# A fourth place in the ring of residual rows of a gated cross-attention block

## The chip, the cores and the metric

The kernel runs on one core of a Trainium2 chip. The metric is the device time of one execution in microseconds (us). Five engines work side by side, each through its own instructions in a fixed order: TensorE (PE, with PEld its weight loads), VectorE (DVE), ScalarE (ACT), GpSimd (POOL) and SyncE (SP), which here only issues DMAs. They wait for one another through semaphores.

## What is computed

The reference is one block of a Flamingo-like network. `x` has 16 sequences of 224 tokens of 512 numbers; the context has 16 sequences of up to 750 rows of 384, of which a mask drops some.

```python
x = x + tanh(g_xattn) * xattn(layernorm(x), ctx, mask, W_q, W_k, W_v, W_o, b_o)
x = x + tanh(g_ffn)   * ffn(layernorm(x), w1, b1, w2, b2)
# xattn: 8 heads of 64; softmax(q k^T / 8, masked) v, then @ W_o + b_o
# ffn:   h = gelu(bitlinear(x, w1, b1)); bitlinear(h, w2, b2)
# bitlinear: rows rms-normalised and rounded to 8 bits, weights rounded to -1, 0, 1
```

Both `x +` are residual adds: the first needs the rows of `x` once more, long after they were normalised for the attention.

## The kernel before, in words

The kernel first sorts the sequences by how many context rows the mask keeps, so that each of 16 attention slots has a fixed width (192, 128 or 64 rows). The work that matters here is in `compact_path`.

The attention goes slot by slot, one sequence of 224 tokens in each. The rest goes by tiles of 128 tokens, two tiles to a pair: 28 tiles, 14 pairs, numbered 0 to 13. Within slot s a list of pieces is merged from three streams by estimated costs: the attention of slot s (`attention_pieces`), the preparation of slots s+1 and s+2 (normalising, gathering context, keys, queries), and `flow`, the work on pairs: the output projection of the newest pair, the first ffn matmul of the pair before it, the second one of the pair before that.

A pair lives like this. `residual(i)` takes a tile `y` of two times 128 rows of 512 numbers, fetches the rows of `x` into it with two indirect DMAs (line 808, through the helper `fetch_x`) and adds `bo`, the projection's bias, on GpSimd (line 1245). `project(i, k)` adds the attention's output on DVE (line 1255). `normalise` makes the 8-bit rows and adds `b2` to `y` on GpSimd (line 1312). `up`, `gelu` and `down` are the ffn: `hp` (line 1333), `h`, the rounded rows `hq`, their transpose `hqT` by a DMA of SP (line 1377), and `fp` (line 1475). `store(i, k)` adds the ffn's output to `y` on DVE (line 1488) and sends the 128 rows out with an indirect DMA of GpSimd (line 1494); the last two pairs go out by SP.

`y` comes from a ring: the tag "y" of the pool `rows` has `bufs` places, and a new tile takes the place of the tile `bufs` pairs before it. The first instruction that writes into a place waits until the store of its old rows has landed. The pool opens when the raw weights of the ffn have been used up, and takes their memory; beside "y" it has tags "hq" (the places of `fx` and `hq`, three) and "hqT" (two).

In the attention, `scores(s, n)` makes the scores `sim` on PE, the exponentials `p` on ACT and the reciprocals `rec` of their sums on DVE, and then scales `p` on GpSimd (line 1140). `turn_probs` transposes the scaled `p` on PE (`ptp`, line 1163, and `ptr`, line 1170).

The pieces are not the last word on the order. When the program is built, a scheduler settles the order of instructions on each engine: an instruction may move ahead of others on its engine if what it needs is there sooner. In the built program of before, GpSimd fetches the rows of pairs 0, 1 and 2 together, as soon as the pool `rows` has its memory, and those of pair i directly behind the second store of pair i-3, whose place they take.

Of the kernel before, what the change touches and what calls it, by code (L numbers as in the profile page):

```python
# [8 lines left out]
F32 = mybir.dt.float32  # L9
# [725 lines left out]
def compact_path(ctx, tc, sh, x, context, out, late_loads, stages):  # L735
# [4 lines left out]
    P = 128  # L740
    B, S, D = x.shape
# [65 lines left out]
    def fetch_x(dst, t):  # L807
        nc.gpsimd.indirect_dma_start(
            out=dst,
            out_offset=None,  # L810
            in_=x_rows,
            in_offset=bass.IndirectOffsetOnAxis(ap=token(t), axis=0),
            bounds_check=B * S - 1,
            oob_is_err=False,
        )
# [420 lines left out]
    late = {}  # L1236

    def residual(i):

        f = pairs[i] = {}  # L1240
        f["y"] = y = late["rows"].tile([P, 2, D], F32, tag="y", name=f"y_{i}", bufs=3)
        for k in range(2):
            fetch_x(y[:, k, :], 2 * i + k)
        for k in range(2):
            nc.gpsimd.tensor_tensor(y[:, k, :], y[:, k, :], sh.bo, ALU.add)
# [471 lines left out]
    for s in range(B):  # L1717
# [8 lines left out]
        if s < 2:  # L1726
            flow = weight_pieces(s)
        else:
            complete = 256 * (projected + 1) <= S * s
            if projected == 0:  # L1730
                nc.gpsimd.tensor_scalar(sh.bo, sh.bo, sh.tgates[:, 0:1], None, ALU.mult)
                nc.gpsimd.tensor_scalar(sh.b2, sh.b2, sh.tgates[:, 1:2], None, ALU.mult)
            if complete:
                flow.append((0.0, lambda i=projected: residual(i)))
            if s == B - 1:
                flow += last_slot(projected)
            elif raised < projected:
                flow += up_pieces(raised)
                raised += 1
            if complete and s < B - 1:  # L1740
                flow += project_pieces(projected)
                projected += 1
                if lowered < raised:
                    flow += down_pieces(lowered)
                    lowered += 1
# [26 lines left out]
    }  # L1772
    i = NPAIR - 1
    residual(i)
    with tc.issue_after(late["av"]), tc.issue_after(late["rounded"]):
        for k in range(2):
# [4 lines left out]
    f = pairs[i - 1]  # L1781
# [80 lines left out]
```

## Time and profile before

| | |
|---|---|
| runs of the kernel before | median 727.38 us of 3 (724.31 to 728.94) |
| the profiled execution | 728.15 us, span of its instructions 726.0 us |
| busy, PE / DVE / ACT / POOL | 674.0 / 493.1 / 413.0 / 391.5 us |
| mean granted TensorE clock | 0.986 |
| residual fetches, line 808 into `y` | 28, median 1035 ns on GpSimd, first at 103.5 us, last at 650.7 us |
| their adds of `bo`, line 1245 | 28, median 1273 ns |
| row stores by GpSimd, line 1494 | 24, median 1115 ns |

A row of a timeline has the start in us from the span's start, the duration in us, the engine, the line of the kernel, the operation with output and input, the count, and in brackets the idle time of the engine before it and what ended that idle time. A row of waits has engine, line and what was waited for, then the total in us, how many times, and the longest. "issue" means that nothing in the profile explains the gap. `p`, `y` and other names stand for all buffers of that name.

### The profile page before, as it was taken

The page shows a single profiled execution, that of the slowest core. Times are in us where ns is not written, and L with a number is a line of the kernel's source. Part 1 is how long each engine was busy: PE and PEld are TensorE (multiplying, and loading weights), DVE is VectorE, ACT ScalarE, POOL GpSimd, SP SyncE. Part 2 cuts the span into 40 slices and gives each one's busy share as a digit, 9 for nine tenths or more (in the row PEclk, how much of TensorE's full clock was granted, in tenths as well). Part 3 has the DMA queues.
Part 4 walks back from the last instruction along what each step waited for, and adds up shares of the span by engine and source line. Part 5 has one row for each costly group of instructions (what it writes and reads, how often), then busy time and mean ns, then how long its engine had stood idle before and what let it go on. Part 6 is the DMA issues. An engine that isn't in the chain of part 4 may idle for free.

```text
span 726.0 us, 11445 instructions
## 1 busy us (share of the span) xinstructions
PE 674.0 (93%) x3917; PEld 430.3 (59%) x3917; DVE 493.1 (68%) x1296; ACT 413.0 (57%) x974; POOL 391.5 (54%) x545
## 2 busy tenths in 40 slices
PE   4996899999989999999798999999999999999984
PEld 3774686765656555656565566566666556554432
DVE  5495666777477476675575966757859393869993
ACT  2556664377484672674566646837556563656642
POOL 5584478553494444735646656457554535276441
PEclk9998999999999999999999999999999999999998
DMA  7784031022232122213232331312313222142211
GB/s 239 288 277 162 0 84 51 18 60 53 68 85 60 54 59 59 85 29 90 60 45 90 83 78 46 66 44 74 82 46 59 73 54 77 30 99 47 69 33 49
DMA packets 80146, 56.74 MB, mean 78 GB/s; under 512 B 68208, under 2 KB 68352, under 8 KB 79952
## 3 DMA queue, kind: packets, MB, share of 16 engines
q1 hardware_dynamic: 72336, 31.22, 18.1%
q0 software_dynamic: 7744, 24.71, 11.1%
q8 instruction: 33, 0.54, 0.3%
q14 instruction: 33, 0.27, 0.1%
HBM read 32.06 MB, written 7.34 MB: 54 GB/s over the span
## 4 chain that ended last, share of the span: by engine, by line
PE 56%; DVE 13%; issue 13%; POOL 10%; ACT 4%; DMA 2%; POOLq 0%; DVEq 0%
PE qp L1066 10%; PE op L1252 9%; PE hp L1333 8%; PE fp L1475 6%; PE kp L946 4%; PE sim L1106 4%; PE vp L962 4%; PE ptp L1163 3%; PE av L1188 2%; DVE a L1369 2%; POOL p L1140 2%; POOL out_dram L1494 1%; DVE hq L1372 1%; PE xnp L1045 1%; POOL y L1312 1%
## 5 line engine op out<-in xcount | busy, mean ns | idle before, releaser
L1140 POOL TENSOR_TENSOR p<-p,rec 112x768 f32<-112x768 f32 (+2 forms) x64 | 78.6, 1230 | 74.9 <-DVE rec L1139 28.8
L1130 ACT ACTIVATE p<-p,nm 112x192 f32<-112x192 f32 (+2 forms) x256 | 104.7, 412 | 9.9 <-DVE nm L1120 6.8
L1066 PE MATMUL qp<-xnT,wq_sb 128*128 128x224 f32 x512 | 105.3, 359 | 0.6 <-issue 0.6
L1252 PE MATMUL op<-wo_sb,xoT 128*128 128x512 f32 x224 | 104.0, 599 | 0.0
L1475 PE MATMUL fp<-w2T,hqT 128*128 128x512 fp8e4 x448 | 101.4, 379 | 2.4 <-ACT hqT L1355 1.3
L1333 PE MATMUL hp<-w1T,xqT 128*128 128x512 fp8e4 x416 | 99.7, 384 | 3.0 <-DVE nm L1120 1.3
L1066 PEld LDWEIGHTS qp<-xnT,wq_sb 128*128 128x128 f32 x512 | 97.1, 194 | 6.4 <-issue 4.1
L1341 DVE SCALAR_TENSOR_TENSOR h<-hp,c,b_bc 128x1024 f32<-128x1024 f32 x52 | 66.5, 1280 | 43.8 <-PE hp L1333 43.5
L1120 DVE CUSTOM_DVE_ANT_0 p<-sim,mask 112x192 f32<-112x192 f32 (+2 forms) x224 | 56.0, 303 | 31.9 <-PE sim L1106 31.5
L1475 PEld LDWEIGHTS <-hqT 128*128 128x128 bf16 x448 | 42.7, 98 | 56.3 <-issue 5.3
L1369 DVE TENSOR_REDUCE a<-h 128x1 f32<-128x2048 f32 x26 | 59.3, 2281 | 20.3 <-ACT h L1366 20.1
L1333 PEld LDWEIGHTS <-xqT 128*128 128x128 bf16 x416 | 40.0, 98 | 47.6 <-issue 8.9
L1252 PEld LDWEIGHTS op<-wo_sb,xoT 128*128 128x128 f32 x224 | 40.6, 190 | 38.3 <-issue 35.9
L1488 DVE SCALAR_TENSOR_TENSOR y<-fp,c,y 128x512 f32<-128x512 f32 x28 | 20.8, 745 | 62.1 <-PE fp L1475 59.3
L1494 POOL DMA_INDIRECT out_dram<-y,token x24 | 27.6, 1148 | 58.0 <-DVE y L1488 53.6
L946 PE MATMUL kp<-ctxT,wk_sb 128*128 128x192 f32 (+1 forms) x360 | 57.8, 308 | 0.0
L1382 ACT ACTIVATE h<-h 128x2048 f32<-128x2048 f32 x25 | 47.7, 1909 | 17.1 <-DVE hq L1372 11.8
L1312 POOL TENSOR_TENSOR y<-y,b_bc 128x512 f32<-128x512 f32 x28 | 37.0, 1322 | 37.2 <-DVE fx L1292 36.9
L781 ACT COPY pT<-ptp 128x448 f32<-128x448 f32 (+1 forms) x62 | 32.2, 535 | 42.2 <-PE ptp L1163 41.4
L946 PEld LDWEIGHTS kp<-ctxT,wk_sb 128*128 128x128 f32 x360 | 52.4, 193 | 5.5 <-issue 3.8
L1106 PE MATMUL sim<-kT,qT 64*112 64x192 f32 (+2 forms) x512 | 51.5, 314 | 1.8 <-issue 0.9
L781 ACT COPY qT<-qp 128x448 f32<-128x448 f32 x29 | 15.4, 532 | 65.9 <-PE qp L1066 60.3
(199 smaller groups left out, 1249.3 us busy)
## 6 DMA issues: line engine op xcount, KB each, us to landing
raw<-in_L_ffn_w_dram SPq DMA_DIRECT2D x16, 512.0 KB
wq_sb<-in_L_xattn_W_q_dram SPq DMA_DIRECT2D x1, 1024.0 KB
b_bc<-in_L_ffn_b_dram SPq DMA_DIRECT2D x1, 1024.0 KB
wk_sb<-in_L_xattn_W_k_dram SPq DMA_DIRECT2D x1, 768.0 KB
wv_sb<-in_L_xattn_W_v_dram SPq DMA_DIRECT2D x1, 768.0 KB
wo_sb<-in_L_xattn_W_o_dram SPq DMA_DIRECT2D x1, 512.0 KB
wo_sb<-in_L_xattn_W_o_dram SPq DMA_DIRECT2D x2, 256.0 KB
out_dram<-y SPq DMA_DIRECT2D x2, 256.0 KB
```

The lines of the kernel that those rows point to most:

```text
L946: nc.tensor.matmul(pk[:, p - p0, :], lhsT=sh.wk[:, c, p * P : (p + 1) * P], rhs=st["ctxT"][:, c, :cap], start=(c == 0), stop=(c == NC - 1),)
L1066: nc.tensor.matmul(pq[:, i, :], lhsT=sh.wq[:, d, (p + i) * P : (p + i + 1) * P], rhs=st["xnT"][:, d, :], start=(d == 0), stop=(d == ND - 1),)
L1106: nc.tensor.matmul(sim[:, j, i, :cap], lhsT=st["qT"][j * DH : (j + 1) * DH, p, q * TQ : (q + 1) * TQ], rhs=keys["kT"][j * DH : (j + 1) * D ...
L1120: nc.vector.tensor_tensor_reduce(out=probs[:, h, :cap], in0=sim[:, j, i, :cap], in1=keys["mask"][:, first + j * begin : first + j * begin ...
L1130: nc.scalar.activation(probs[:, h, :cap], probs[:, h, :cap], AF.Exp, bias=nmax, scale=-1.0, accum_out=total[:TQ, h : h + 1],)
L1140: nc.gpsimd.tensor_tensor(probs[:, :, first : first + cap], probs[:, :, :cap], rec[:TQ].unsqueeze(2).to_broadcast([TQ, 4, cap]), ALU.mult,)
L1252: last = nc.tensor.matmul(po, lhsT=xoT[:, d, at : at + P], rhs=sh.wo[:, d, :], start=(d == 0), stop=(d == ND - 1))
L1333: last = nc.tensor.matmul(ph[:, n, :], lhsT=f["xqT"][:, k * ND + d, :], rhs=w1T[:, d, at : at + NB], start=(d == 0), stop=(d == ND - 1),)
L1341: nc.vector.scalar_tensor_tensor(h[:, cols], ph.rearrange("t i n -> t (i n)"), f["c1", k], sh.b1[:, cols], ALU.mult, ALU.add)
L1369: nc.vector.tensor_reduce(amax[:, k : k + 1], h, AX.X, ALU.max, apply_absolute_value=True)
L1382: nc.scalar.activation(f["h", k], f["h", k], AF.Square, accum_out=ss[:, k : k + 1])
L1475: last = nc.tensor.matmul(po, lhsT=f["hqT", k][:, n, :], rhs=w2T[:, n, :], start=(n == 0), stop=(n == NF - 1))
```

## The change

One number: the tag "y" of the pool `rows` has four places instead of three.

```diff
@@ residual(i) @@
         f = pairs[i] = {}
-        f["y"] = y = late["rows"].tile([P, 2, D], F32, tag="y", name=f"y_{i}", bufs=3)
+        f["y"] = y = late["rows"].tile([P, 2, D], F32, tag="y", name=f"y_{i}", bufs=4)
         for k in range(2):
             fetch_x(y[:, k, :], 2 * i + k)
```

A place is 4 KB in each of the 128 partitions. Pair i now takes the place of pair i-4 instead of pair i-3. The pool grows by one place, and the tags behind "y" lie one place further on. No computation is added or removed.

## The prediction

> **What bounds the kernel now.** I read the page first (busy shares, then the chain that ended last), then the waits, then the timeline of GpSimd (POOL) around the residual rows, and last TensorE (PE) beside it. The two lines of the page:
>
> ```profile
> PE 674.0 (93%) x3917; PEld 430.3 (59%) x3917; DVE 493.1 (68%) x1296; ACT 413.0 (57%) x974; POOL 391.5 (54%) x545
> ...
> PE 56%; DVE 13%; issue 13%; POOL 10%; ACT 4%; DMA 2%; POOLq 0%; DVEq 0%
> ```
>
> PE is busy for 674.0 of 726.0 us, so all its idle time together is 52 us. A microsecond taken from another engine counts only where PE was waiting for it, and one added counts only where PE comes to wait. The list of waits tells how GpSimd enters:
>
> ```profile
> PE ptp L1163 <- POOL p L1140: 16.9, 10, 5.6
> ...
> POOL y L808 <- DMA out_dram<-y,token: 20.4, 10, 2.3
> ```
>
> GpSimd stands 20.4 us in ten places before it may fetch residual rows, because the store of the rows that lie in the place hasn't landed. PE waits 16.9 us for the scaled probabilities `p` of line 1140, which GpSimd makes behind those fetches. One such place, in GpSimd's timeline (start, duration, what, idle before it):
>
> ```profile
> 192.97 1.11 POOL L1494 DMA_INDIRECT out_dram<-y,token  x1 [6.37 <-DVE y L1488]
> 196.13 1.06 POOL L808 DMA_INDIRECT y<-in_x_dram,token  x1 [2.05 <-DMA out_dram<-y,token]
> 197.50 1.02 POOL L808 DMA_INDIRECT y<-in_x_dram,token  x1 [0.31 <-issue]
> 199.62 1.27 POOL L1245 TENSOR_TENSOR y<-y,bo_bc 128x512 f32<-128x512 f32 x1 [1.11 <-DMA y<-in_x_dram,token]
> 200.85 1.46 POOL L1140 TENSOR_TENSOR p<-p,rec 112x768 f32<-112x768 f32 x1
> ```
>
> Store of pair 0, 2.05 us of standing, fetch of pair 3 into pair 0's place, 1.11 us of standing for the fetched rows, the add, and only then `p`. The change's words aim at the 2.05 us.
>
> [...]2.05 us from the end of the store's issue at 194.08 to the fetch. [...]the wait stands in GpSimd's queue, and everything behind it stands too. [...]the fetch of 196.13 shows 1.06 us, and its reader starts at 199.62, 3.49 us after the fetch began.
>
> **The change part by part.** The order in which the two programs issue their instructions decides this case. On PE, DVE, ACT and SP it is the same. On GpSimd only the residual fetches and their adds of `bo` move: every one stands one pair earlier. Before, the fetches of pairs 0, 1 and 2 stand together at the start, and pair i's stands directly behind the second store of pair i-3. After, pairs 0 to 3 stand together at the start, and pair i's stands directly behind the second store of pair i-4. With four places pair i takes the place of pair i-4. So the fetch again takes the place whose rows were sent in the instruction before it, and the wait for that store's semaphore is still on it. The extra place has been used to fetch a pair sooner, not to keep a place empty.
>
> 1. *The ten middle places* (pairs 0 to 9 stored): store, standing, two fetches, standing, add, `p` in the same order as in the excerpt, with the same tile sizes. Change: 0. Whether the rows are of pair 3 or 4 is nothing to `p`, and the first reader of the rows (line 1255) is a whole pair further off than before.
>
> 2. *The start* gets the two fetches and two adds of pair 3:
>
> ```profile
> 111.09 1.02 POOL L808 DMA_INDIRECT y<-in_x_dram,token  x1 [0.16 <-issue]
> 112.14 2.50 POOL L1245 TENSOR_TENSOR y<-y,bo_bc 128x512 f32<-128x512 f32 x2
> 114.80 1.01 POOL L808 DMA_INDIRECT y<-in_x_dram,token  x1 [0.16 <-issue]
> 115.85 1.29 POOL L1245 TENSOR_TENSOR y<-y,bo_bc 128x512 f32<-128x512 f32 x1
> 118.29 1.33 POOL L1245 TENSOR_TENSOR y<-y,bo_bc 128x512 f32<-128x512 f32 x1 [1.15 <-DVE keys L869]
> 119.58 1.46 POOL L1140 TENSOR_TENSOR p<-p,rec 112x768 f32<-112x768 f32 x1
> 121.90 1.47 POOL L1140 TENSOR_TENSOR p<-p,rec 112x768 f32<-112x768 f32 x1 [0.86 <-DVE mv_x L1011]
> ```
>
> The idle 1.15 us is the landing of the fetch of 114.80 (114.80 + 3.49 = 118.29), whatever name stands beside it. The new order is: fetch pair 2 second half, fetch 3, add 2, fetch 3, add 2, add 3, add 3, `p`. With 1.02 us and a gap of 0.31 or 0.16 for a fetch, 1.27 for an add and 3.49 from issue to landing: fetch at 114.80; fetch of 3 at 116.12 to 117.12; add to 118.45; fetch at 118.6 to 119.6; add at 119.65 to 120.95; third add to 122.2 (its rows landed at 119.6); fourth add, rows landed at 118.6 + 3.49 = 122.1, to 123.45. Then the two `p`: 123.45 to 124.9 and 124.95 to 126.4. They end 3.9 and 3.0 us later than before. It is 5.1 us of work (2 x 1.02, 2 x 0.25, 2 x 1.27), of which the 1.15 us of idle time takes up one.
>
> PE comes to the first of these `p` here:
>
> ```profile
> 121.50 0.92 PE L946 MATMUL kp<-ctxT,wk_sb 128*128 128x192 f32 x4
> 122.65 0.29 PE L1163 MATMUL ptp<-ident,p 112*128 112x112 f32 x1 [0.22 <-DVE y L1255]
> 122.77 1.48 PE L946 MATMUL kp<-ctxT,wk_sb 128*128 128x192 f32 x8
> 124.08 0.45 PE L1163 MATMUL ptp<-ident,p 112*128 112x112 f32 x3
> 124.38 0.35 PE L1170 MATMUL ptr<-ident,p 112*128 112x112 f32 x2
> 124.57 0.55 PE L1163 MATMUL ptp<-ident,p 112*128 112x112 f32 x4
> ```
>
> It can start at 124.9 + 0.06 (the gap from `p` to PE at 206.3) instead of 122.65: 2.3 us of new idle time. The second `p` is wanted at 124.57 + 2.3 = 126.9 and is done at 126.4: no more. What else is behind on GpSimd, the normalising of x tile 4 and the gather of context 5 (124.71 and 126.40 before), is read by PE from 148 on, and GpSimd then stood 3.38 us before its next `p` at 132.17. So only PE's 2.3 us are lost, and since the chain runs through PE from 122.93 to 152, nothing gives them back. Bounds: 1.2 us (landing sooner, adds lying better) to 3.9 us (the whole lateness of `p`).
>
> 3. *The end* loses the fetch of pair 13 behind the store of pair 10:
>
> ```profile
> 645.67 1.10 POOL L1494 DMA_INDIRECT out_dram<-y,token  x1 [0.17 <-DVE nm L1120]
> 648.79 1.06 POOL L808 DMA_INDIRECT y<-in_x_dram,token  x1 [2.01 <-DVE rec L1139]
> 649.87 0.62 POOL L1140 TENSOR_TENSOR p<-p,rec 112x256 f32<-112x256 f32 x1
> ```
>
> That `p` could go 1.1 us sooner (its `rec` ends at 648.72), and two adds at 652.29 and 654.94 vanish. But PE starts the transposes of this `p` at 650.92 directly behind line 1333's matmuls of 649.19, without idle time, and the next `p` at 658.19 waits for DVE. Gain 0, at most the 0.77 us that PE waits at 662.60.
>
> 4. *Places in memory*: the rows pool is 4 KB longer, so the buffers of tags hq and hqT lie one place on; the first transpose of `hqT` on SP gets one more wait, for GpSimd work long done by then. Cost 0. The page shows no effect of addresses; I keep half a microsecond either way.
>
> Sum: 0 + 2.3 - 0 + 0 = +2.3 us. The profiled execution took 728.15 us (span 726.0), so 730.45. The median of the runs is 727.38, 0.77 lower: 729.7.
>
> **The rivals.**
> - *A, forecast*: later `p` at the start costs PE 2.3 us, carried to the end: 729.7, its own range 728.5 to 731.5. Chance 0.55.
> - *B, hidden*: PE takes it back in later waits, or the freed GpSimd time at the end pays for it. For it: 52 us of PE idle time, 0.77 of them at 662.60. Against it: the later waits for `p` hang on stores that follow PE's own matmuls, so they move along. 727.4, give or take one. Chance 0.22.
> - *C, slower*: the crowding at the start also pushes the second `p`, the x tile and the gather, and PE pays the full 5.1 us of work plus a late stage behind it: 727.4 + 5 to 8, 733 to 735. For it: GpSimd is 74% busy from 100 to 120. Against it: GpSimd's 3.38 us of idle time before 132.17. Chance 0.15.
> - *D, faster, the change does what its words say*: the wait at the fetch is gone because the place was emptied a pair ago. Then each GpSimd stall of about 2 us goes, and PE gets back what it waits just behind, up to 2.05 a time: 1.07, 1.39, 1.47, 2.05 (of 3.65), 1.17, 0.35, 0.43, 1.02, together 8.95 us: 718.5. It decides as soon as more than 2.3 us of this come back. Against it: in the built order pair 4's fetch stands right behind the store of pair 0, with the wait. Chance 0.08.
>
> **How the numbers follow.** Likeliest is A: 729.7. The range goes from B's lower end to C's lower part, 726 to 733.5, which also holds the 0.6% by which the runs of before differ. About 1% (7.3 us) is what a measurement of this kernel tells from no change: over 1% faster is D alone, 0.08; over 1% slower is C's upper end and what the trace doesn't show of buffer places, 0.12; the rest, 0.80, lies within.
>
> **What would show it.** Right: in the profile after, ten waits of line 808 for `out_dram<-y`, still near 2.0 us each (about 20 in total); eight residual fetches before 125 us instead of six; PE waiting some 2 us for `p` of line 1140 near 123, and later stages later by that much. No residual fetch after 620. Wrong: if that wait is gone or far under 15 us in total, step 1 fails; if PE shows no wait near 123, step 2; if the time falls by over 3 us, something in the middle moves that the order doesn't show.

## The result, and the profile after

The changed kernel takes 730.86 us (median of 13 runs, 726.09 to 732.42); the kernel before, beside it, 726.4 us (13 runs, 723.4 to 728.94). The ratio is 1.0055, 95% interval 1.0037 to 1.0073: about 4.0 us slower, within 1%; the two medians alone differ by 4.5 us. The profiled execution took 731.07 us with a span of 729.0 us.

The two lines of the page after:

```profile
PE 677.2 (93%) x3917; PEld 433.4 (59%) x3917; DVE 498.2 (68%) x1296; ACT 412.8 (57%) x974; POOL 388.5 (53%) x545
...
PE 66%; DVE 14%; issue 6%; POOL 6%; ACT 4%; DMA 2%; POOLq 0%; DVEq 0%; ACTq 0%
```

PE is busy 3.2 us longer and DVE 5.1 us longer for the same numbers of instructions. Nothing was added to either, so something made instructions longer; 3.3 of DVE's 5.1 us are six instructions shown below. The list of waits after:

```profile
PE ptp L1163 <- POOL p L1140: 12.8, 10, 3.7
PE ptp L1163 <- DVE y L1255: 3.5, 1, 3.5
...
POOL y L808 <- DMA out_dram<-y,token: 20.5, 10, 2.2
```

The ten waits for a store are all there, 20.5 us against 20.4. The 3.5 us for DVE's line 1255 are new. (The longest wait for `p` before, 5.6 us, lay near 62 us, ahead of any residual row, where it is 1.5 us in the changed kernel and 2.8 us in `y3_late` below. Single executions differ there, so I compare stretches behind it.) The middle place in GpSimd's timeline, to be laid beside the one of before:

```profile
197.00 1.11 POOL L1494 DMA_INDIRECT out_dram<-y,token  x1 [6.36 <-DVE y L1488]
200.13 1.06 POOL L808 DMA_INDIRECT y<-in_x_dram,token  x1 [2.02 <-DMA out_dram<-y,token]
201.50 1.03 POOL L808 DMA_INDIRECT y<-in_x_dram,token  x1 [0.31 <-issue]
203.76 1.27 POOL L1245 TENSOR_TENSOR y<-y,bo_bc 128x512 f32<-128x512 f32 x1 [1.23 <-DMA y<-in_x_dram,token]
204.99 1.47 POOL L1140 TENSOR_TENSOR p<-p,rec 112x768 f32<-112x768 f32 x1
```

Same order, same 2.0 us: the fetch now is pair 4's, and it still stands right behind the store that empties its place. So the loss is made elsewhere, at the start. GpSimd there:

```profile
113.68 1.01 POOL L808 DMA_INDIRECT y<-in_x_dram,token  x1 [0.16 <-issue]
115.00 1.00 POOL L808 DMA_INDIRECT y<-in_x_dram,token  x1 [0.30 <-issue]
116.03 1.28 POOL L1245 TENSOR_TENSOR y<-y,bo_bc 128x512 f32<-128x512 f32 x1
117.47 1.11 POOL L808 DMA_INDIRECT y<-in_x_dram,token  x1 [0.16 <-issue]
118.60 3.71 POOL L1245 TENSOR_TENSOR y<-y,bo_bc 128x512 f32<-128x512 f32 x3
122.28 1.46 POOL L1140 TENSOR_TENSOR p<-p,rec 112x768 f32<-112x768 f32 x1
```

The first `p` ends at 123.74. TensorE should start its transpose 0.06 us later, but does so 1.4 us later still, and not for `p` (`kp` are the keys of a later slot, `qp` its queries):

```profile
120.70 0.92 PE L946 MATMUL kp<-ctxT,wk_sb 128*128 128x192 f32 x4
125.17 0.31 PE L1163 MATMUL ptp<-ident,p 112*128 112x112 f32 x1 [3.55 <-DVE y L1255]
125.29 2.77 PE L946 MATMUL kp<-ctxT,wk_sb 128*128 128x192 f32 x8
...
129.41 2.92 PE L1066 MATMUL qp<-xnT,wq_sb 128*128 128x224 f32 x14
```

It waits 3.55 us, and the eight `kp` matmuls behind take 2.77 us where they took 1.48. DVE's timeline says why line 1255 was late:

```profile
117.36 6.80 DVE L846 TENSOR_SCALAR ind<-place,upto 125x192 bf16<-125x192 bf16 x6
124.09 0.16 DVE L1139 RECIPROCAL rec<-sum 112x4 f32<-112x4 f32 x1
...
124.31 0.71 DVE L1255 SCALAR_TENSOR_TENSOR y<-op,tgates,y 128x512 f32<-128x512 f32 x1
```

Six small instructions, the indicators with which a later context's rows are selected, took 6.80 us (3.48 us before). The view of line 846 alone, in the stretch around it (shortest/median/longest in ns), shows that one of them took nearly all of it, here in the changed kernel,

```profile
L846 DVE TENSOR_SCALAR ind<-place,upto x6: 253/254/5907, 117.4 to 123.9; 125x192 bf16<-125x192 bf16 x6
```

and here in the kernel before:

```profile
L846 DVE TENSOR_SCALAR ind<-place,upto x6: 251/253/1499, 118.2 to 121.4; 125x192 bf16<-125x192 bf16 x6
```

The long one began at about 117.9 and was let go when `p` ended at 123.74 (the last of the six starts at 123.9). And the table by stretches (the last four columns: GpSimd's busy time, the granted TensorE clock, DMA share, GB/s) has the clock of the changed kernel behind the gap at 0.72, where the kernel before has 1.00:

```profile
118.00:124.00 6.00, 3.62 (x15) 1.94 (x13) 6.00 (x3) 1.72 (x7) 5.71 (x5) 1.00 0.13 46
124.00:130.00 6.00, 4.83 (x23) 4.66 (x24) 2.72 (x8) 1.72 (x4) 5.12 (x7) 0.72 0.01 3
```

### The profile page after: what moved, and what is told of

The parts are those of the page before. It is cut to its first block, busy times and chain, and to the rows that moved or that the text cites. A ratio compares the mean times of both kernels' runs of the same rounds, so it can differ in the third digit from the quotient of the medians.

```text
span 729.0 us, 11445 instructions
## 1 busy us (share of the span) xinstructions
PE 677.2 (93%) x3917; PEld 433.4 (59%) x3917; DVE 498.2 (68%) x1296; ACT 412.8 (57%) x974; POOL 388.5 (53%) x545
## 4 chain that ended last, share of the span: by engine, by line
PE 66%; DVE 14%; issue 6%; POOL 6%; ACT 4%; DMA 2%; POOLq 0%; DVEq 0%; ACTq 0%
PE qp L1066 11%; PE op L1252 10%; PE fp L1475 9%; PE hp L1333 9%; PE kp L946 5%; PE vp L962 5%; PE sim L1106 5%; PE ptp L1163 3%; PE av L1188 3%; DVE a L1369 2%; POOL p L1140 2%; DVE hq L1372 1%; PE xnp L1045 1%; DMA hqT<-hq 1%; PE ctxp L935 1%
## 5 line engine op out<-in xcount | busy, mean ns | idle before, releaser
L946 PE MATMUL kp<-ctxT,wk_sb 128*128 128x192 f32 (+1 forms) x360 | 61.0, 319 | 0.0
L946 PEld LDWEIGHTS kp<-ctxT,wk_sb 128*128 128x128 f32 x360 | 55.5, 201 | 5.4 <-issue 3.8
```

Of the source, the lines that this page charges most:

```text
L946: nc.tensor.matmul(pk[:, p - p0, :], lhsT=sh.wk[:, c, p * P : (p + 1) * P], rhs=st["ctxT"][:, c, :cap], start=(c == 0), stop=(c == NC - 1),)
```

## The experiments

Three theories. T1: `p` is late, and nothing else. T2: on top of that GpSimd's row of operations without a gap keeps DVE from running, so DVE's line 1255, which `ptp` waits for as well (the wait of 3.55 us above), ends after `p`; and TensorE's clock drops behind the gap (0.72 against 1.00). T3: the time is lost elsewhere, in moved buffers or in the middle. Then a fourth question: what is the change worth if it does what its words say?

The measure for the start is the stretch from the `kp` matmuls ahead of the gap to the first `qp` behind it, each row's start taken from the PE timeline: before 125.46 - 121.50 = 3.96 us, changed 129.41 - 120.70 = 8.71 us. All runs are put together in one table below.

### Is it the start, and which part of it

`y3_late`: pair 3's fetches and adds behind the last `p` of slot 3. The scaling of `p` records its instruction in `late["scaled", s, n]`; `issue_after` sets the order within the engine only.

```diff
-        for k in range(2):
-            fetch_x(y[:, k, :], 2 * i + k)
-        for k in range(2):
-            nc.gpsimd.tensor_tensor(y[:, k, :], y[:, k, :], sh.bo, ALU.add)
+        with ExitStack() as held:
+            if i == 3:
+                held.enter_context(tc.issue_after(late["scaled", 3, 3]))
+            for k in range(2):
+                fetch_x(y[:, k, :], 2 * i + k)
+            for k in range(2):
+                nc.gpsimd.tensor_tensor(y[:, k, :], y[:, k, :], sh.bo, ALU.add)
```

> Four places as in the changed kernel, but the two fetches and two adds of pair 3 are issued behind the last scaled p of slot 3 instead of at the start; nothing else on any engine changes its place. If the loss is the crowded start: near the kernel before, 726 to 727.5 us, no wait of TensorE of more than about 1 us for ptp near 122 us, qp at about 124.5 to 125.5 us (129.41 in the changed kernel, 125.46 before), the clock in 124 to 130 us back near 1.0, and the longest instruction of the indicators (line 846, near 118 us) at 1.5 us or less. If the loss comes from the moved buffers or from the fetches in the middle that belong to a later pair: still about 730.

Measured: 1.0007 of before (0.9992 to 1.0022), the stretch 3.80 us, no wait of `ptp`, and the indicators as before:

```profile
L846 DVE TENSOR_SCALAR ind<-place,upto x6: 256/257/1503, 115.9 to 118.9; 125x192 bf16<-125x192 bf16 x6
```

Within this interval all of the loss is in these four instructions' place. The buffers lie as in the changed kernel, and the later fetches stand as there, with ten waits for a store, 20.6 us in total: T3 falls.

`add3_late`: the two fetches stay, only the adds are held (the `with` covers the second loop alone).

> Pair 3's two fetches stay at the start, its two adds are issued behind the last scaled p of slot 3. GpSimd then has 2 x (1.02 + 0.25) us more than before ahead of p, of which the idle 1.15 us takes part: p ends near 121.3 us. Late p alone: PE comes to ptp at about 121.9 to 122.6, after p, so nothing is lost, 726 to 727. VectorE blocked by GpSimd's row of operations: the indicators go on only when p has ended, the 1.3 us of VectorE's work behind them end near 122.6, PE loses up to 0.8 us, 726.5 to 727.5, and the longest instruction of line 846 is 2.5 to 3.5 us. If it is the fetches and not the adds that cost: near 730.

Measured: 1.0008 (0.9993 to 1.0023). `p` ended at 116.88 + 1.47 = 118.35, and TensorE waited 1.17 us, for DVE and not for `p`:

```profile
119.60 0.29 PE L1163 MATMUL ptp<-ident,p 112*128 112x112 f32 x1 [1.17 <-DVE y L1258]
```

The longest indicator took 3437 ns, between the 1.5 us of before and the 5.9 us of the changed kernel. The stretch is 4.91 us, so 0.95 us were lost in this execution; the runs can't tell that from nothing. At most 1.7 us (0.0023 of 725) are lost with the fetches at the start, so most of the loss needs the two adds there. That a wait for DVE outlasts `p` already here speaks for T2.

### Another form for the indicators: three runs that missed

The next guess was that the form of DVE's instruction decides whether it is held beside GpSimd's. Two other ways of writing the indicators try it: `one_port` (the label is a guess at the cause, which no run shows), whose source is a copy of the row of places in three runs of 64 with gaps, and `accum`, the accumulating form (the old source, with `ALU.add` and `accum_out=sh.count[:, n : n + 1]`). Of `one_port`, without the lines that fill `sh.gaps`:

```diff
+                if s == 5:
+                    nc.vector.tensor_scalar(
+                        ind[:, n, :].rearrange("p (a c) -> p a c", a=3), sh.gaps[:TJ, :, :64],
+                        sh.upto[:, n, b : b + 1], None, ALU.is_ge)
+                    continue
```

> The changed kernel with the same order on every engine, but the six indicators of context 5 (line 846, near 118 us) read a copy of the row of places that lies in three runs of 64 with gaps[...]. One iota at the start is new. If VectorE was blocked by GpSimd[...]: none of these six takes more than about 0.4 us, VectorE's line 1255 ends by 120 us, PE then waits for p alone (end 123.7) and starts ptp at about 123.8 instead of 125.17: 1.4 us less idle time, and with a shorter gap perhaps less of the slow clock: 728 to 730 us, qp at 127 to 128.3. If the 5.9 us have another cause (a wait for a semaphore, an uneven record): they stay, ptp stays at 125.2, and the time at 730 to 731.

> The changed kernel with the one-port indicators once more, beside the changed kernel itself. Blocked VectorE: 1.5 to 3 us under the changed kernel of this call, PE idle 2.2 to 2.5 us with GpSimd's p as the releaser, the clock near 1.0 behind it. [...]

> The changed kernel in the same order, but the six indicators of context 5 (line 846 before, near 118 us) are written in the form of the instruction that also gives a sum, into a column that nobody reads. [...] The source in three runs with gaps did not do that: its instructions were as long as the others (256 ns) and were blocked as long. [...]no one of the six over 0.7 us, VectorE's line 1255 long done when PE comes to ptp, PE idle 2.2 to 2.5 us for GpSimd's p and never 3.5 for VectorE, so the late p alone is left: 1.003 to 1.004 of before. If something else holds them: one of them again at 3.2 or 5.9 us.

Measured: 1.0034 (1.0019 to 1.005), 1.0077 (1.0052 to 1.0102) and 1.0086 (1.0052 to 1.0121). The edit sat at the wrong context. The indicators near 118 us are those of context 6; the rewritten ones of context 5 run near 80 us, where the view by line finds them at 292 to 305 ns (gaps) and 391 to 405 ns (accumulating). Near 118 us these three kernels are the changed kernel, so the conclusion in the expectation of `accum`, that the gaps did not help, was drawn from instructions that had not been touched. What the runs do give is three more profiles of the changed order there, beside two repeats of the changed kernel itself:

> The changed kernel once more, for a second profile on the chip of the runs beside it. If the blocking of VectorE is the rule and not an accident of one execution: the longest of line 846's instructions near 118 us again 5 to 6.5 us, PE again idle about 3.3 to 3.6 us ahead of ptp with VectorE's line 1255 as the releaser, the clock in the 6 us behind it again under 0.85, and 1.004 to 1.007 of the kernel before. If it was an accident: a longest instruction of 1.5 us and about 1.003 of before.

> The changed kernel a third time, beside the accumulating one on the same chip. Four profiles of the changed order so far: the longest indicator at 5.91, 3.25, 3.24 and 5.87 us, PE's idle time ahead of ptp 3.55, 2.45, 2.38 and 3.60 us. If VectorE is let in at one of the ends of GpSimd's instructions by chance: one of these two values again, with the idle time that goes with it, and 1.003 to 1.006 of before.

Measured: 1.0038 (1.002 to 1.0055) and 1.0086 (1.0064 to 1.0107). In six profiles of this order there are two outcomes. In four the longest indicator takes 5.87 to 5.91 us and TensorE waits 3.55 to 3.60 us for DVE; in two it takes 3.25 and 3.24 us, and TensorE waits only 2.45 and 2.38 us, for `p`. Here is one of the two, `after_again`, on PE and on GpSimd:

```profile
120.92 0.32 PE L1163 MATMUL ptp<-ident,p 112*128 112x112 f32 x1 [2.45 <-POOL p L1140]
```

```profile
115.73 3.72 POOL L1245 TENSOR_TENSOR y<-y,bo_bc 128x512 f32<-128x512 f32 x3
119.40 2.88 POOL L1140 TENSOR_TENSOR p<-p,rec 112x768 f32<-112x768 f32 x2
```

The last of its six indicators starts at 118.2, where the second of the three adds ends (115.73 + 2 x 1.24); in the other outcome DVE is let in only where `p` ends (123.74 in the changed kernel). So in these six profiles DVE got in at one of the ends of GpSimd's instructions, and at the first in none. What decides which, no run shows.

### The same at the right context

The two edits with `s == 6`. The order of all other instructions is that of the changed kernel.

> As the accumulating kernel before, but now at the right context: the six indicators that run near 118 us are those of context 6. The two kernels that rewrote context 5 changed instructions near 80 us, where they took 402 ns (accumulating) and 298 ns (three runs with gaps) in place of about 255, and left those near 118 us alone. Expected[...]: all six at about 0.4 us, line 1255's result over a microsecond before PE wants it, PE idle 2.2 to 2.6 us with GpSimd's p as the releaser, never 3.5 with VectorE; the time 1 to 3 us under the changed kernel (1.002 to 1.005 of before). If something other[...] holds them: again one of 3.2 or 5.9 us and 1.004 to 1.009.

> The indicators of context 6, near 118 us, read the row of places in three runs with gaps (298 ns each at 80 us, where 255 are usual[...]). [...]all six at about 0.3 us, PE idle 2.2 to 2.6 us for GpSimd's p alone, 1.002 to 1.005 of before, as with the accumulating form. [...]

Measured: `accum6` 1.0016 (1.0001 to 1.0031), just under the 1.002 to 1.005 expected, `one_port6` 1.0029 (0.9998 to 1.0061). The changed kernel was not measured beside them, so how much time they gain over it is not shown; the profiles show what they change. The view by line, first of `accum6`, then of `one_port6`:

```profile
L848 DVE TENSOR_SCALAR_CACHE_REDUCE ind<-place,upto x6: 397/400/402, 118.7 to 120.3; 125x192 bf16<-125x192 bf16 x6
```

```profile
L849 DVE TENSOR_SCALAR ind<-gaps,upto x6: 290/291/292, 115.5 to 116.6; 125x192 bf16<-125x192 bf16 x6
```

In `accum6` the adds run from 119.82, so half of the indicators lie beside them, and none is longer for it. In `one_port6` the six are done by 116.9, ahead of the adds, and only a fetch (115.94 to 116.95) lies beside them; in the changed kernel the long one began beside a fetch too (at about 117.9, the fetch 117.47 to 118.58). TensorE then waits for `p` alone, in `accum6`

```profile
125.02 0.32 PE L1175 MATMUL ptp<-ident,p 112*128 112x112 f32 x1 [2.09 <-POOL p L1152]
```

and in `one_port6`

```profile
122.16 0.31 PE L1174 MATMUL ptp<-ident,p 112*128 112x112 f32 x1 [2.39 <-POOL p L1151]
```

T1 is the part that is left: 2.1 to 2.4 us. The accumulating form was not held beside adds (402 ns at most, where the plain form took up to 5.91 us), in one profile of each kernel; the source in runs was not held beside a fetch (292 ns at most), and beside adds it wasn't seen. Why the form matters, no run shows. The table, with the clock of the 6 us stretches 118 to 124 and 124 to 130:

| kernel | longest indicator, us | PE idle ahead of `ptp`, us | for | clock | `kp` to `qp`, us |
|---|---|---|---|---|---|
| before | 1.50 | 0.22 | DVE | 1.00, 1.00 | 3.96 |
| `y3_late` | 1.50 | 0 | | 1.00, 1.00 | 3.80 |
| `add3_late` | 3.44 | 1.17 | DVE | 1.00, 1.00 | 4.91 |
| `accum6` | 0.40 | 2.09 | `p` | 1.00, 1.00 | 5.85 |
| `one_port` | 3.24 | 2.38 | `p` | 1.00, 1.00 | 6.13 |
| `after_again` | 3.25 | 2.45 | `p` | 0.83, 0.88 | 7.25 |
| `one_port6` | 0.29 | 2.39 | `p` | 0.91, 0.81 | 7.50 |
| `after_third` | 5.87 | 3.60 | DVE | 1.00, 0.72 | 8.24 |
| changed | 5.91 | 3.55 | DVE | 1.00, 0.72 | 8.71 |
| `one_port_again` | 5.87 | 3.60 | DVE | 0.81, 0.90 | 8.69 |
| `accum` | 5.91 | 3.60 | DVE | 0.95, 0.77 | 8.69 |

Three steps can be read off: late `p`, 1.9 to 2.2 us over before; a blocked DVE, 1.2 us more idle time (3.6 against 2.4); a slow clock, 1.1 to 1.4 us more (7.25 and 7.50 against 6.13 at the same idle time). With the 3.96 us of before they add up to 8.2 to 8.8, and the four rows that have all three took 8.24 to 8.71. Every row with a gap of 3.5 us or more has the slow clock, the rows with about 2.4 us have it in two of three, those with 2.09 us or less have not.

How long the slow clock lasts can be read too. In the changed kernel's profile the clock is 0.50 from 125.31 to 128.72 us, for 3.41 us, and 1.00 on both sides. In the rows for 118 to 130 us that is 0.28 missing of 6 us, and 0.28 x 6 / 0.5 = 3.4 us; the sum over both stretches gives 3.4 to 3.5 us in every slowed row. In this profile the clock falls to 0.50 at 43.39, 67.28, 87.76, 125.31, 354.00 and 722.64 us, and these starts lie 7, 6, 11, 67 and 108 times 3.413 us apart; in that of before it falls at 60.96, 88.26, 351.09 and 719.73 us, 8, 77 and 108 times apart. But for the one at the program's end, each of these slow stretches lasts one or two such steps. In the changed kernel TensorE works for 0.14 us in the step ahead of 125.31. In `after_again` most of the gap of 2.45 us falls into the 3.41 us ahead of the slow stretch, which have 1.08 us of work (the rows have the stretch, its length, the busy times of PE, PEld, DVE, ACT and POOL, the clock, DMA share, GB/s):

```profile
118.59:122.00 3.41, 1.08 (x7) 1.08 (x8) 2.48 (x6) 0.00 (x0) 3.41 (x3) 1.00 0.00 0
122.00:125.42 3.42, 3.42 (x17) 3.29 (x16) 1.02 (x2) 1.73 (x4) 2.97 (x7) 0.50 0.02 5
```

In `one_port` the rows divide the gap of 2.38 us between two stretches, the emptier one with 1.58 us of work, and the clock stays up:

```profile
116.19:119.60 3.41, 2.87 (x13) 1.57 (x12) 3.41 (x2) 0.91 (x4) 3.38 (x4) 1.00 0.28 77
119.60:123.02 3.42, 1.58 (x11) 1.56 (x12) 1.99 (x6) 0.00 (x0) 3.33 (x4) 1.00 0.00 0
123.02:126.43 3.41, 3.31 (x24) 3.10 (x23) 1.01 (x2) 1.67 (x4) 3.04 (x6) 1.00 0.02 5
```

That the place of the gap on the steps made the difference is a reading of these rows; no run moved a gap to test it. How much work in a step keeps the clock up isn't fixed either: in the changed kernel's profile a step with 2.87 us of TensorE's work (39.98 to 43.39) stands ahead of a slow one, and a step with 1.77 us (698.74 to 702.16) ahead of a fast one.

### What the words of the change would be worth

`hold4_store2` has four places, but keeps the fetch where it stood before; the place it takes was sent a pair ago. The first add follows it, the second add follows the next `p`. The lines that hold the fetch (`...` marks what is left out, among it the line that holds the second add):

```diff
...
+            if i > 2:
+                held.enter_context(tc.issue_after(late["stored", i - 3, 1]))
             for k in range(2):
                 fetch_x(y[:, k, :], 2 * i + k)
...
```

> Four places, and every fetch from pair 3 on is issued behind the second store of pair i-3, where it stood in the kernel before; its first add follows it and its second add follows the next p. The place it takes was sent a whole pair ago, which is what the change's words say. Expected on GpSimd: the ten waits of about 2 us for the store are gone (20 us in all down to under 2), p comes about 2 us sooner each time, the 1.1 us for the fetched rows stay. If PE gets its waits back as my case D has it: 717 to 720 us. If part is absorbed by the next wait (VectorE, ScalarE, or a lower clock): 720 to 725. If p was not what PE waited for: 726 to 727.

Measured: 721.22 us, 0.9944 (0.9929 to 0.9958), about 4.1 us faster than before, the second of the three cases expected. No wait of line 808 for a store is left. Its middle place:

```profile
188.82 1.11 POOL L1502 DMA_INDIRECT out_dram<-y,token  x1 [6.37 <-DVE y L1496]
190.24 1.06 POOL L808 DMA_INDIRECT y<-in_x_dram,token  x1 [0.30 <-issue]
...
193.84 1.28 POOL L1249 TENSOR_TENSOR y<-y,bo_bc 128x512 f32<-128x512 f32 x1 [1.22 <-DMA y<-in_x_dram,token]
195.08 1.46 POOL L1140 TENSOR_TENSOR p<-p,rec 112x768 f32<-112x768 f32 x1
```

From the store to `p` it is 6.26 us, against 7.88 before. TensorE's waits for `p` from 200 us on are 6.67 us in total here and 11.32 us before: 4.65 us less. My case D had counted 8.95. Two things were wrong in its sum. The waits of 0.35, 0.43 and 1.02 us did not shrink with the store's wait gone (they are 1.03, 0.43 and 1.02 here). And at the longest one, the wait ahead of the first `p` shrank from 3.65 to 0.56 us, but 2.70 us came up ahead of the second. Between the two `p` stand the fetches of `x`, as before, and the second add of 1.27 us, which this kernel has moved there:

```profile
338.45 0.60 PE L1163 MATMUL ptp<-ident,p 112*128 112x112 f32 x4 [0.56 <-POOL p L1140]
...
343.67 0.79 PE L1163 MATMUL ptp<-ident,p 112*128 112x112 f32 x4 [2.70 <-POOL p L1140]
```

`hold4_p` and `hold3_p` go further: fetches and adds stand behind the second `p` after the store, with four and with three places, in one and the same order (`slot_of[i - 2] + 1` is the slot whose `p` follow the store of pair i-3). The line that sets it:

```diff
+            if i > 2:
+                held.enter_context(tc.issue_after(late["scaled", slot_of[i - 2] + 1, 1]))
```

> Four places, and each fetch from pair 3 on is issued behind the second p that follows the store of pair i-3, with its adds behind it, so that neither the wait for the store nor the fetches, their landing and the adds stand ahead of p. Issuing at the store's place gave 0.9944. If PE still waits behind the fetches and adds: 1 to 3 us more, 718 to 720.5 (0.990 to 0.993), PE's waits for p in the slots with a store under 2 us in all except where x is fetched between two p. If the first p was no longer what PE waited for: 0.994 to 0.995. If the fetches now crowd x's normalising or the gather behind p: 722 to 726.

> The same order of instructions with three places. The fetch then takes the place whose rows were sent two p ago, some 4 us and more after the store's issue, so its store (about 2 us) has landed. If only the distance in GpSimd's queue between store and fetch counts: the same time as with four places, within 0.7 us, and no wait of line 808 for the store. If the fourth place is needed: waits of line 808 of up to 2 us come back, and 2 to 5 us more than with four.

Measured: four places 720.6 us, 0.9928 (0.9902 to 0.9953); three places 722.12 us, 0.995 (0.9931 to 0.9969). The intervals overlap. The medians differ by 1.5 us, more than the 0.7 us that would have meant the same time and less than the 2 us that would have meant a need for the fourth place. Neither waits for a store at line 808, and in both TensorE's waits for `p` are small, with four places and then with three:

```profile
PE ptp L1163 <- POOL p L1140: 4.6, 6, 1.1
```

```profile
PE ptp L1163 <- POOL p L1140: 5.4, 6, 1.4
```

With three places, from the store to `p`:

```profile
188.44 1.11 POOL L1499 DMA_INDIRECT out_dram<-y,token  x1 [6.37 <-DVE y L1493]
193.61 1.46 POOL L1140 TENSOR_TENSOR p<-p,rec 112x768 f32<-112x768 f32 x1 [4.07 <-PE hp L1338]
```

Now `p` waits for its own inputs, 5.17 us behind the store's start, so 2.7 of the 7.88 us of before were there to be had. (The view names `hp`, but `rec`, which `p` is scaled with, ended at 193.46, just ahead of `p`.) Both kernels beat the two of this case. How far `hold4_p` is ahead of `hold4_store2`, and whether four places beat three at all, these runs don't settle. They show that the order alone, with three places, gains 0.3 to 0.7% over before.

## Why the prediction was right or wrong

Predicted were 729.7 us and 2.3 us of loss, 0.80 for within 1%. Measured were 730.86 us and 4.0 us: inside the range, within 1%, and lost where the likeliest case put it, at the start. That 729.7 lies so near is in part luck. It was counted from 727.4 us for the kernel before, which took 726.4 beside the changed one, so the loss itself is 1.7 us over the forecast. By its steps:

1. *The ten middle places, 0*: right. Ten waits, 20.5 us in total, the `p` waits at 1.17, 1.42, 1.48, 3.67, 0.97, 0.37, 0.43 and 1.02 us against 1.07, 1.39, 1.47, 3.65, 1.17, 0.35, 0.43 and 1.02.
2. *The start, +2.3 us*: the term that was too small. The lateness of `p` was sized well: GpSimd's row runs as predicted (from the fetch at 113.68 to the end of the first `p` 10.06 us, predicted 10.1), and TensorE lost 2.1 to 2.4 us to `p` wherever DVE was ready. But "only PE's 2.3 us are lost" left out two things: the blocked DVE with up to 1.2 us and TensorE's slow clock with 1.1 to 1.4 us. In the profiled execution the start lost 8.71 - 3.96 = 4.75 us, over the upper bound of 3.9, and the sign that was named, some 2 us of waiting for `p` near 123, is there as 3.55 us of waiting for DVE. The first of the two was in reach: the rows of before show `ptp` with "0.22 <-DVE y L1255", so DVE had no slack, and six indicators of 253 ns that took 3.48 us. The chain of work that ended last, which the prediction took up at 122.93 on PE, came to that point through DVE (start and us on the chain, engine, tile, line):

```profile
118.24 2.64 DVE ind L846 x3
...
121.03 0.61 DVE ind L846 x3
...
121.86 0.65 DVE y L1255
...
122.65 0.29 PE ptp L1163
```

3. *The end, 0*: right. The last residual fetch starts at 616.5 us, and TensorE waits the same 0.77 us for `p` at 665.72 as before at 662.60.
4. *Places in memory, 0*: not contradicted; `y3_late` has the same places, and its interval is 0.9992 to 1.0022.

Of the rivals, B would have needed the loss to be taken back. About 0.9 us of it was: TensorE's wait of 0.94 us ahead of `hp`, at 214.49 in the kernel before, is gone after, and no more came back. The lead of before goes from 3.95 us at `qp` (the changed kernel had 0.80 us in hand at the `kp` ahead of the gap) to 3.06 at 306 us and 3.16 at 711 us. C had 5 to 8 us, from the second `p`, the x tile and the gather; the loss stayed under that, and these three were not late for anyone: TensorE has no gap between 132 and 155 us. D did not happen, and where it was made to happen it was worth 4.1 us, not 8.95.

The three measurements of the changed kernel are 1.0055, 1.0038 and 1.0086, and the intervals of the last two don't meet. Nor do those of the two measurements of `one_port` on one chip, 1.0034 (1.0019 to 1.005) and 1.0077 (1.0052 to 1.0102). In the first of these ten of the 20 runs took 724.3 to 726.8 us, ten 728.5 to 731.1, and none lies between. That fits the two outcomes at DVE and at the clock, in different mixtures, but one execution of each measurement has a profile, so this is argued and not shown.

## What to carry to other kernels

In this kernel one more place in the ring did not take the fetch away from the store that it waits for: the scheduler issued the fetch a pair sooner, and the wait stayed, until the order was held as well. Ask of every place added what the instruction that fills it will then wait for, and what stands behind it in its queue. And when work is added to GpSimd, look not only at who waits for GpSimd, but at which DVE instructions lie beside it (here an indicator of 253 ns was held for 5.9 us), at what is queued behind those, and at TensorE's clock behind the gap (here 0.50 for 3.4 us behind a gap of 3.55 us).

## What the runs showed of the hardware that I had not expected

- One indicator of 253 ns was held for 5.9 us, from within a fetch through three adds and a scaling by GpSimd that followed each other without a gap. Not every end of a GpSimd instruction let DVE in: of these five ends DVE took the last in four profiles of the changed order, and the third in two.
- Behind a gap of 2.4 us TensorE ran for about 3.4 us at half its clock in two profiles of three (3.42 us at 0.50 in `after_again`), which cost 1.1 to 1.4 us on top of the gap. In the third, `one_port`, the clock stayed at 1.00.
- The same six indicators take 253 ns each in the plain form, 291 ns with a source in three runs, and 400 ns accumulating. In the slower forms they are done sooner here.
